# A selective-scan layer on one core: B and C loaded to 64 partitions and copied to the other 64 by ScalarE, u loaded in two halves

## The chip, the core and the metric

The kernel runs on one core of a Trainium2 chip. The metric is the device time of one execution in microseconds (us); lower is better. Engines are named as in the profile: PE is TensorE's matmul side and PEld its weight loads, DVE is VectorE, ACT is ScalarE, POOL is GpSimd, SP is SyncE, which only issues DMAs here.

## The reference, cut to what matters

The network has four layers on an input of 2 x 128 x 128 x 128 (images, channels, rows, columns): a Mamba layer (layer 0), a gate made from 8 x 8 windows (layer 1), a second Mamba layer of the same form (layer 2) and a residual block of two 3x3 convolutions (layer 3). The change is in the Mamba layers alone. After a 3x3 convolution, the 128 channels of every pixel are read as a sequence of 8 tokens with 16 features:

```python
seq = y.reshape(B * H * W, 8, 16)
xz = einsum('nld,ed->nle', seq, in_proj_w); xi, z = split(xz, 2)     # 32 inner channels each
xc = silu(causal_conv4(xi) + conv1d_b)
dt, Bm, Cm = split(einsum('nld,ed->nle', xc, x_proj_w), [1, 17])     # 1, 16 and 16 wide
dt = softplus(einsum('nlr,dr->nld', dt, dt_proj_w) + dt_proj_b)
dA, dBx = exp(dt[..., None] * A), dt[..., None] * Bm[:, :, None, :] * xc[..., None]
h = dA * h + dBx;  y_t = sum(h * C_t, over the 16 states)            # scan over the 8 tokens
out = einsum('nld,ed->nle', (y + D * xc) * silu(z), out_proj_w)
```

Each pixel has its own sequence, with a state h of 32 inner channels x 16 states. After the layer comes a group norm, SiLU and the residual.

## The kernel before, in words

One tile is 4 image rows, 512 pixels; `_mamba` handles 64 tiles for each of the two layers, numbered k. The state of a token is a tile of 128 partitions x 4 x 512: the 32 inner channels are split into 4 groups j (`NJ`, on the free axis) of 8 channels e (`DJ`), and the 128 partitions are the 8 channels e x 16 states n. Which partition holds which (e, n) is told by `_state` (L72), and the constant matrices `neg`, `red` and `alog` are laid out by it.

For every tile, PE and ACT make xc, z, dt, B and C, all with pixels on the free axis, through one PSUM buffer `one`: a matmul writes it, ACT copies it out, and the next matmul may start. POOL makes u = dt * xc (L374). As u, B and C are needed on other partitions than where they arise, `store` (L376) writes them to scratch in DRAM (`su` and `sb`, ten DMAs), and `load` (L429) reads them back for each of tokens 0 to 6, replicated over partitions: u to all 16 states n (`ur`, 128 x 4 x 512), and B and C to all 8 channels e (`bcr`, 128 x 2 x 512). Before the change a load is four DMAs on SP, in this order: u to partitions 0 to 111 (L435), u to 112 to 127 (L436), B and C to 0 to 111 (L439), B and C to 112 to 127 (L440). `ur` has 3 buffers, `bcr` 5.

Then, for each token t:

- `inject` (L442, POOL, instruction L445) makes h_t = ur * B, for t = 0 to 6, in one instruction of 128 x 2048. `h` has 4 buffers.
- `decay` (L447), for t = 1 to 7: eight matmul pieces (L454) spread dt over the partitions and scale it by A, into two PSUM tiles `set` of 128 x 1024; ACT takes exp of each (L463). There are three `set` buffers, so ACT can be at most one and a half tokens ahead of DVE.
- `token` (L465), twice per token, once for each half of the 2048 columns: DVE multiplies the set by the state before (L472), multiplies that by C into `r` (L473) and, but for the last token, adds the injected part (L477).
- `gather` (L485): PE sums `r` over the states into `ys` (L492).

`gate` (L501, DVE instruction L505), `out` (L507, with L512 and L520), `spread` (DVE, L523) and `keep` (SP, L527) finish a tile.

The order on every engine is written by hand: each step is put on a list with a due time in tokens, tile k adding 7k (`SPAN`); the list is sorted, and each engine runs its part of it in that order. In a due time t is the token. What matters here: `load` is due at t - 3.7, `inject` at t - 1.8, `decay` at t - 1.2, `token` at t - 1. Around the end of a tile's scan ACT therefore has, in this order and partly for the next tiles: exp of token 6 (both halves), the copy of z's second half (L354), a table load, SiLU of xc and of z (L357), the copy of B (L407), a table load, exp of token 7, a copy of dt (L365), the copy of C (L407), exp of the next tile's token 1, a second copy of dt (L365). On the next token's period follow copies of `t` (L421) and of `o` (L520), exp of token 2, a table load, softplus (L368), a table load and exp of token 3. PE's matmuls L400 (for B and C), L364 (for dt) and L454 stand between these, each waiting for ACT to clear `one`.

SP's DMAs signal on eight semaphores in turn, and an issue waits for the DMA eight before it to land; so at most eight DMAs, two loads, are under way.

Of the kernel before, what the change touches and what calls it, by code (L numbers as in the profile page):

```python
# [31 lines left out]
P = 128  # L32
NT, FT = 8, 16
DI, DS, DC = 32, 16, 4
NQ = 4
NJ = DI * DS // P
DJ = DI // NJ
NG = 4
CG = P // NG
WIN = 8  # L40
ROWS = 4
NS = ROWS * P
# [7 lines left out]
def _constants(H):  # L50

    parts = {}

    neg = np.zeros((NJ, NQ, DJ, NQ, P), np.float32)
    red = np.zeros((P, NQ, NQ, DJ), np.float32)
    gsum = np.zeros((2, NQ, DS, 2, NJ, NQ, DJ), np.float32)
    for q in range(NQ):
        for e in range(DJ):
            neg[:, q, e, q, _state(e)] = -1.0
            red[_state(e), q, q, e] = 1.0  # L60
        for g in range(2):
            gsum[g, q, :, g, :, q, :] = 1.0
    parts["neg"] = neg.reshape(P, -1)
    parts["red"] = red.reshape(P, -1)
    parts["gsum"] = gsum.reshape(P, -1)
    parts["group"] = np.kron(np.eye(NG), np.full((CG, CG), 1.0 / CG)).astype(np.float32)
    parts["ident"] = np.eye(P, dtype=np.float32)
    parts["neghalf"] = np.full((P, CG), -0.5, np.float32)
    return _packed(parts)


def _state(e):  # L72


    return np.arange(DS) + P - DS if e == DJ - 1 else np.arange(DS) * (DJ - 1) + e


def _bilinear(n):
# [38 lines left out]
def _mamba_layout(w):  # L117
# [5 lines left out]
    def half(a):  # L123

        a = a.reshape(*a.shape[:-2], 2, NQ, NJ, DJ)
        return np.ascontiguousarray(np.swapaxes(a, -3, -2)).reshape(*a.shape[:-4], 2 * P)
# [18 lines left out]
    for q in range(NQ):  # L145
        pdt1[:, q, :, :, q, :] = by_d[0][:, :, None, None]
        pdt2[:, q, :, :, q, :] = w["dt_proj_w"][:, 0].reshape(NJ, DJ)[None, None, :, :]
        pb[:, q, :, q, :] = by_d[1 : 1 + DS].transpose(1, 2, 0)
        pc[:, q, :, q, :] = by_d[1 + DS :].transpose(1, 2, 0)
        for e in range(DJ):  # L150
            alog[:, q, e, q, _state(e)] = w["A_log"].reshape(NJ, DJ, DS)[:, e, :]
# [126 lines left out]
OWN_AT = (-6.3, -5.8)  # L278
U_AT, OWN_U_AT = -5.0, -4.3
STORE_AT = -4.15  # L280
LOAD_AT, INJECT_AT = -3.7, -1.8
REP_AT = -1.2
SUM_AT = 0.35
D_AT = (1.25, 4.2)
# [4 lines left out]
def _mamba(tc, src, w, con, dst, scratch, stats, H):  # L289


    nc = tc.nc
# [11 lines left out]
    live = {}  # L304
# [124 lines left out]
    def load(k, t):  # L429

        s = live[k]
        n = P - DS
        ur = s["ur", t] = st.tile([P, NJ, NS], F32, tag="ur", name="ur", bufs=3)
        u = s["su"][t]
        nc.sync.dma_start(out=ur[:n], in_=u[: DJ - 1].unsqueeze(0).to_broadcast([DS, DJ - 1, NJ, NS]))  # L435
        nc.sync.dma_start(out=ur[n:], in_=u[DJ - 1].unsqueeze(0).to_broadcast([DS, NJ, NS]))  # L436
        m = s["bc", t] = st.tile([P, 2, NS], F32, tag="bcr", name="bcr", bufs=5)
        b = s["sb"][t]
        nc.sync.dma_start(out=m[:n], in_=b.unsqueeze(1).to_broadcast([DS, DJ - 1, 2, NS]))  # L439
        nc.sync.dma_start(out=m[n:], in_=b)  # L440

    def inject(k, t):  # L442
        s = live[k]
# [90 lines left out]
    def taps(k, a, b):  # L534
        return [(k, conv, tap) for tap in range(a, b)]
# [11 lines left out]
    x1, z1 = ahead(1)[0], behind(1)[0]  # L547
    order = [(0, band)] + taps(0, 0, 9) + [(0, turn)] + x0 + taps(1, 0, 3) + dt0 + taps(1, 3, 5) + bc0
    order += [(0, load, 0), (0, load, 1), (0, load, 2)]
    order += z0 + taps(1, 5, 9) + [(1, turn), (0, decay, 1), (0, inject, 0), (0, inject, 1)] + own0  # L550
    order += x1[:2] + z1[:2]
    early = {x: n - 100.0 for n, x in enumerate(order)}

    def put(k, at, f, *args):
        at = early.get((k, f, *args), k * SPAN + at)
        todo.append((at, len(todo), f, (k, *args)))


    for k in range(len(src) * ntile):
        if k * ROWS % BAND == 0:  # L560
            put(k, BAND_AT, band)
        for tap in range(9):
            put(k, CONV_AT[tap], conv, tap)
        put(k, TURN_AT, turn)
        for n in range(4):
            put(k, IN_AT[n], project, *divmod(n, 2))
        for name in ("xc", "zs"):
            put(k, SILU_AT, silu, name)
        for i in range(2):
            put(k, BC_AT[i], inout, i)  # L570
        for g in range(2):
            put(k, DT_AT[g], step, g)
        put(k, SOFTPLUS_AT, softplus)
        put(k, PROD_AT, product)
        put(k, U_AT, scaled)
        for g in range(2):
            put(k, OWN_AT[g], own, g)
        put(k, OWN_U_AT, own_u)
        put(k, STORE_AT, store)
        for t in range(NT - 1):  # L580
            put(k, LOAD_AT + t, load, t)
            put(k, INJECT_AT + t, inject, t)
        for t in range(1, NT):
            put(k, REP_AT + t, decay, t)
            for jp in range(2):
                put(k, t - 1 + jp / 2, token, t, jp)
            put(k, SUM_AT + t, gather, t)
        for g in range(2):
            put(k, D_AT[g], through, g)
            put(k, V_AT[g], gate, g)  # L590
        put(k, OUT_AT, out)
        put(k, STATS_AT, spread)
        put(k, KEEP_AT, keep)
# [26 lines left out]
def _gates(tc, src, w, con, y, stats, wm, b1, up, dst, H):  # L620
# [6 lines left out]
    with tc.tile_pool(name="dg", bufs=2) as dp, tc.tile_pool(name="dg1", bufs=1) as sp, tc.tile_pool(  # L627
# [58 lines left out]
        def gram(b, y0):  # L686
# [3 lines left out]
            pg = s["pg"] = psg.tile([P, 2, 512], F32, tag="pg", name="pg")  # L690
            tiles = [(a, a * P // 2, g * CG) for g in range(NG) for a in range(2)]
            for a, pa, c0 in tiles:
# [335 lines left out]
def _program(ctx, tc, d, cols, out):  # L1028
# [7 lines left out]
    with tc.tile_pool(name="const", bufs=1) as cp, tc.tile_pool(name="wts", bufs=1) as wp:  # L1036
        cc = cols["const"]
        ct = cp.tile([P, cc["neghalf"][1]], F32, tag="ct", name="ct")
        nc.sync.dma_start(out=ct, in_=d["const"])
        con = {k: ct[:, a:b] for k, (a, b) in cc.items()}  # L1040
        w1 = cp.tile([P, CG], F32, tag="w1", name="w1")
        nc.sync.dma_start(out=w1, in_=d["w1t"])
        w2 = cp.tile([CG, 2 * P + P // 2], F32, tag="w2", name="w2")
        nc.sync.dma_start(out=w2, in_=d["w2b"])
        b1 = cp.tile([CG, 1], F32, tag="b1", name="b1")
        nc.sync.dma_start(out=b1, in_=d["b1"])
        wm = {"w1": w1, "w2": w2[:, :P], "b2": w2[:, P : 2 * P], "one": w2[:, 2 * P :]}

        y = [dram.tile([P, H, P], F32, tag=f"y_{b}", name=f"y_{b}") for b in range(B)]

        def layer(src, n):
            w = _layer_weights(nc, wp, {k: d[f"L{n}_{k}"] for k in ("conv", "fold", "alog", "keep")}, cols[n], con)
            stats = wp.tile([P, B, H // ROWS, 6], F32, tag="stats", name="stats")
            _mamba(tc, src, w, con, y, scratch, stats, H)
            return w, stats

        x = [d["x"][b] for b in range(B)]
        w, stats = layer(x, 0)
        _gates(tc, x, w, con, y, stats, wm, b1, d["up"], x2, H)
        w, stats = layer(x2, 2)  # L1060
        with tc.tile_pool(name="ps_n", bufs=1, space=PSUM) as pp:
            norm = [_norm(nc, npool, pp, w, con, stats, b) for b in range(B)]
# [44 lines left out]
```

## Time and profile before

| what | value |
|---|---|
| time, median of 3 runs | 7559.09 us (7551.93 to 7567.43) |
| span of the profiled execution | 7571.5 us |
| DVE busy in the span | 7011.8 us (93%) |
| POOL, PE, ACT busy in the span | 73%, 83%, 57% |
| DMA | 1769.80 MB, mean 234 GB/s |
| layer 0's scan, first to last DVE token instruction | 57 to 3307 us |
| layer 2's scan | 3655 to 6899 us |

The profiled execution has no separate time of its own; its span is 12.4 us above the median of the three runs, so a profiled microsecond is taken as a run's microsecond, and differences are added to the median. The profile gives, for each engine, its busy time, the groups of instructions by source line with the idle time just before them and what ended it ("releaser"), a table of waits, a timeline of instructions, and tables of busy time by window with the granted TensorE clock and the share of time that the 16 DMA engines were busy. The scan stages of the two layers are 6493 us of the span and the rest is the gate layer, the residual block and the start.

### The profile page before, as it was taken

Reading aid. Unit: us, or ns where it says so; the run is one execution under the profiler, and the core shown is the slowest. Engines: PE = TensorE matmul, PEld = TensorE weight load, DVE = VectorE, ACT = ScalarE, POOL = GpSimd, SP = SyncE. Lnnn points to the kernel's source line nnn. Section 1 sums busy time; section 2 is a strip of 40 time slices with the busy share of each in tenths; the row PEclk is TensorE's granted clock in tenths of the full one; section 3 lists DMA queues with packets and bytes.
Section 4 is the critical chain, followed back from the end, with each engine's and each line's share of the span. In section 5 each row is a group of like instructions: output and inputs, shape, how many; then the busy total and the mean of one; then the engine's idle time right before and its main releaser. Section 6 shows DMA issues by size and latency. Waiting matters only on the chain.

```text
span 7571.5 us, 89536 instructions
## 1 busy us (share of the span) xinstructions
PE 6319.0 (83%) x30416; PEld 2335.1 (31%) x30416; DVE 7011.8 (93%) x7114; ACT 4282.3 (57%) x4877; POOL 5499.8 (73%) x1783
## 2 busy tenths in 40 slices
PE   7888888888888888867788888888888888887994
PEld 2222222222222222224222222222222222223873
DVE  5999999999999999978699999999999999999986
ACT  5666666666656656545556666666656655662222
POOL 5878777877787778754578777877787778775541
PEclk8999999999999999978899999999999999997997
DMA  8999999999999999954799999999999999996604
GB/s 204 252 251 252 251 250 246 256 251 253 246 248 254 250 243 249 245 194 173 193 249 247 250 250 249 250 256 246 249 252 252 251 245 253 249 253 199 207 7 172
DMA packets 573738, 1769.80 MB, mean 234 GB/s; under 512 B 85568, under 2 KB 239712, under 8 KB 458208
## 3 DMA queue, kind: packets, MB, share of 16 engines
q1 hardware_dynamic: 568672, 1747.28, 88.1%
q10 hardware_dynamic: 4608, 16.78, 0.6%
q8 instruction: 242, 3.96, 0.2%
q14 instruction: 216, 1.77, 0.1%
HBM read 1552.83 MB, written 210.89 MB: 233 GB/s over the span
## 4 chain that ended last, share of the span: by engine, by line
DVE 41%; DMA 25%; PE 19%; issue 7%; ACT 5%; POOL 2%; SPq 1%; POOLq 0%; DVEq 0%; ACTq 0%
DMA bcr<-sb 19%; DVE set L472 14%; DVE h L477 12%; DVE r L473 12%; PE m L911 6%; DMA ur<-su 3%; PE one L350 2%; PE set L454 2%; ACT set L463 2%; PE ys L492 2%; PE one L400 2%; POOL h L445 2%; DVE v L505 1%; PE ys L483 1%; ACT xc L357 1%
## 5 line engine op out<-in xcount | busy, mean ns | idle before, releaser
L445 POOL TENSOR_TENSOR h<-ur,bcr 128x2048 f32<-128x2048 f32 x896 | 4060.7, 4539 | 1257.0 <-DMA bcr<-sb 1096.1
L472 DVE TENSOR_TENSOR set<-set,h 128x1024 f32<-128x1024 f32 x1792 | 2193.5, 1224 | 267.6 <-ACT set L463 165.4
L473 DVE TENSOR_TENSOR r<-set,bcr 128x1024 f32<-128x1024 f32 x1792 | 2194.5, 1225 | 61.5
L463 ACT ACTIVATE set<-set 128x1024 f32<-128x1024 f32 x1792 | 1745.9, 1006 | 870.0 <-PE set L454 856.6
L477 DVE TENSOR_TENSOR h<-set,h 128x1024 f32<-128x1024 f32 x1536 | 1866.0, 1215 | 28.1 <-POOL h L445 27.8
L454 PE MATMUL set<-dt,rep 32*128 32x512 f32 x7168 | 1402.9, 675 | 104.9 <-DVE h L477 98.1
L492 PE MATMUL ys<-r,ct 128*32 128x512 f32 x7168 | 1172.5, 635 | 36.4 <-DVE r L473 36.1
L323 PE MATMUL one<-band,conv 128*128 128x512 f32 x2304 | 1081.3, 605 | 21.9 <-DMA band<-in_x_dram 12.6
L454 PEld LDWEIGHTS set<-dt,rep 32*128 32x128 f32 x7168 | 405.1, 193 | 1002.3 <-issue 468.1
L400 PE MATMUL one<-xc,keep 128*64 128x512 f32 x1008 | 322.4, 723 | 462.1 <-ACT xc L357 355.5
L323 PEld LDWEIGHTS one<-band,conv 128*128 128x128 f32 x2304 | 406.6, 189 | 668.0 <-issue 596.8
L911 PE MATMUL m<-comb,u 128*128 128x256 f32 x2304 | 507.8, 381 | 46.0 <-DVE comb L904 44.8
L483 PE MATMUL ys<-t,ct 128*128 128x512 f32 x512 | 322.6, 716 | 252.3 <-DVE v L505 250.7
L911 PEld LDWEIGHTS m<-comb,u 128*128 128x128 f32 x2304 | 436.2, 190 | 117.3 <-issue 54.5
L492 PEld LDWEIGHTS ys<-r,ct 128*32 128x32 f32 x7168 | 181.2, 112 | 929.2 <-issue 759.6
L352 ACT ACTIVATE xc<-one,keep 128x512 f32<-128x512 f32 x252 | 173.4, 688 | 509.2 <-PE one L350 504.2
L374 POOL TENSOR_TENSOR u<-dt,xc 128x1024 f32<-128x1024 f32 x128 | 302.8, 2365 | 98.0 <-ACT dt L368 98.0
L420 PE MATMUL one<-prod,ct 128*128 128x512 f32 x504 | 280.8, 640 | 109.1 <-POOL prod L412 78.8
L350 PE MATMUL one<-y,w_in 128*128 128x512 f32 x504 | 341.1, 765 | 1.6 <-ACT xc L352 1.6
L463 ACT ACT_TABLE_LOAD x254 | 325.9, 1283 | 4.5
L427 POOL TENSOR_TENSOR t<-t,xc 128x1024 f32<-128x1024 f32 x128 | 302.4, 2363 | 10.0
L364 PE MATMUL one<-xc,w_dt 128*128 128x512 f32 x504 | 306.4, 692 | 2.7 <-ACT bc L407 2.7
(167 smaller groups left out, 5901.7 us busy)
## 6 DMA issues: line engine op xcount, KB each, us to landing
ur<-su SPq DMA_DIRECT2D x896, 896.0 KB, 11.5
bcr<-sb SPq DMA_DIRECT2D x896, 448.0 KB, 11.7
ur<-su SPq DMA_DIRECT2D x896, 128.0 KB, 11.1
su<-u SPq DMA_DIRECT2D x1024, 64.0 KB, 3.4
sb<-bc SPq DMA_DIRECT2D x256, 224.0 KB, 2.7
bcr<-sb SPq DMA_DIRECT2D x896, 64.0 KB, 11.0
y<-o SPq DMA_DIRECT2D x128, 256.0 KB, 9.3
band<-in_x_dram SPq DMA_DIRECT2D x28, 640.0 KB, 10.9
```

Of the source, the lines that this page charges most:

```text
L323: nc.tensor.matmul(py.rearrange("p (r w) -> p r w", r=ROWS), lhsT=w["conv"][:, tap, :], rhs=xb[:, r + kh : r + kh + ROWS, kw : kw + P], st ...
L350: nc.tensor.matmul(p, lhsT=w[("in", "z")[i]][:, g, :], rhs=s["y"], start=True, stop=True)
L400: nc.tensor.matmul(p[g * NQ * DS : (g + 1) * NQ * DS, :], lhsT=w[("xb", "xcm")[i]], rhs=s["xc"][:, g, :], start=True, stop=True,)
L445: nc.gpsimd.tensor_tensor(b, s["ur", t], s["bc", t][:, 0].unsqueeze(1).to_broadcast([P, NJ, NS]), ALU.mult)
L454: nc.tensor.matmul(a[j // 2][:, j % 2, :], lhsT=w["rep"][r, q, :], rhs=s["dt"][r, g, :], start=True, stop=True, tile_position=(r.start, 0),)
L463: nc.scalar.activation(x, x, AF.Exp)
L472: nc.vector.tensor_tensor(pt, pt, s["h", t - 1][:, js, :], ALU.mult)
L473: nc.vector.tensor_tensor(s["r", t][:, js, :], pt, s["bc", t - 1][:, 1].unsqueeze(1).to_broadcast([P, 2, NS]), ALU.mult)
L477: nc.vector.tensor_tensor(s["h", t][:, js, :], pt, s["h", t][:, js, :], ALU.add)
L483: nc.tensor.matmul(s["ys", g], lhsT=con["ident"], rhs=s["t1"][:, g, :], start=True, stop=False)
L492: nc.tensor.matmul(s["ys", g][a : a + NQ * DJ, :], lhsT=red[:, q, :], rhs=r[:, j, :], start=False, stop=(q == NQ - 1), tile_position=(0, a),)
L911: nc.tensor.matmul(m[:, n // 2, n % 2], lhsT=u[:, i, kw, :], rhs=v[:, i, :, kw : kw + P], start=(kw == 0), stop=(kw == 2),)
```

## The change

`_state` gets a new order of partitions: channel e and state n sit on partition 64 * (e // 4) + 4 * n + e % 4, so that the lower 64 partitions hold channels 0 to 3 and the upper 64 hold channels 4 to 7. As B and C do not depend on the channel, the two halves of `bcr` are then equal. `load` reads B and C for partitions 0 to 63 only, by two DMAs of 32 partitions whose source has 8 states as its leading dimension, and a new step `double` copies them to partitions 64 to 127 with one ACT instruction of 64 x 1024. u is loaded by two DMAs of 64 partitions, the upper half first; its bytes stay the same. A load still has four DMAs, but B and C now come before u. `double` is due at t - 2.19, just behind the exp of the token before (due at t - 2.2) and ahead of `inject` (t - 1.8), which reads its result, as `token` does.

```diff
+NE = DJ // 2
 def _state(e):
-    return np.arange(DS) + P - DS if e == DJ - 1 else np.arange(DS) * (DJ - 1) + e
+    return P // 2 * (e // NE) + NE * np.arange(DS) + e % NE
...
-LOAD_AT, INJECT_AT = -3.7, -1.8
+LOAD_AT, DOUBLE_AT, INJECT_AT = -3.7, -2.19, -1.8
...
     def load(k, t):
         s = live[k]
-        n = P - DS
+        half, part = P // 2, P // 4
         ur = s["ur", t] = st.tile([P, NJ, NS], F32, tag="ur", name="ur", bufs=3)
-        u = s["su"][t]
-        nc.sync.dma_start(out=ur[:n], in_=u[: DJ - 1].unsqueeze(0).to_broadcast([DS, DJ - 1, NJ, NS]))
-        nc.sync.dma_start(out=ur[n:], in_=u[DJ - 1].unsqueeze(0).to_broadcast([DS, NJ, NS]))
         m = s["bc", t] = st.tile([P, 2, NS], F32, tag="bcr", name="bcr", bufs=5)
-        b = s["sb"][t]
-        nc.sync.dma_start(out=m[:n], in_=b.unsqueeze(1).to_broadcast([DS, DJ - 1, 2, NS]))
-        nc.sync.dma_start(out=m[n:], in_=b)
+        u, b = s["su"][t], s["sb"][t]
+        for at in (0, part):
+            rows = b[at // NE : (at + part) // NE]
+            nc.sync.dma_start(
+                out=m[at : at + part], in_=rows.unsqueeze(1).to_broadcast([part // NE, NE, 2, NS])
+            )
+        for at, e in ((half, NE), (0, 0)):
+            nc.sync.dma_start(
+                out=ur[at : at + half], in_=u[e : e + NE].unsqueeze(0).to_broadcast([DS, NE, NJ, NS])
+            )
+
+    def double(k, t):
+        m = live[k]["bc", t]
+        nc.scalar.copy(m[P // 2 :], m[: P // 2])
...
+            put(k, DOUBLE_AT + t, double, t)
             put(k, INJECT_AT + t, inject, t)
```

In the first tile's hand-made order, `double` of tokens 0 and 1 is put just before the steps that need it.

More of the change, by code (lines that the diff above doesn't have):

```diff
@@ L549, in _mamba @@
     order += [(0, load, 0), (0, load, 1), (0, load, 2)]
-    order += z0 + taps(1, 5, 9) + [(1, turn), (0, decay, 1), (0, inject, 0), (0, inject, 1)] + own0
+    order += z0 + taps(1, 5, 9) + [(1, turn), (0, double, 0), (0, decay, 1), (0, inject, 0), (0, double, 1), (0, inject, 1)] + own0
     order += x1[:2] + z1[:2]
```

## Prediction

> **What bounds the kernel now.** First the table of busy time by window, for a stretch inside layer 2's scan. Columns: window, length, busy us of PE, PEld, DVE, ACT and POOL, granted clock, DMA share, GB/s.
>
> ```profile
> 5000.00:6400.00 1400.00, 1194.37 (x4950) 377.26 (x4942) 1353.10 (x1197) 856.08 (x974) 1109.30 (x322) 0.96 0.98 250
> ```
>
> Two things are nearly full: DVE, 1353 of 1400 us, and the DMA engines, 0.98 of the time at 250 GB/s. A tile takes (3307 - 57) / 64 = 50.8 us, so DVE's 46.9 idle us over 27.6 tiles are 1.7 us per tile: the most that could ever be won is 1.7 x 128 = 218 us, 2.9%. The DMA engines work 0.98 x 50.8 = 49.8 us per tile. Then the waits (engine and line, released by: us in total, times, longest):
>
> ```profile
> POOL h L445 <- DMA bcr<-sb: 1096.1, 406, 14.4
> ...
> DVE set L472 <- ACT set L463: 165.4, 185, 9.3
> ...
> DVE set L472 <- POOL h L445: 97.2, 2, 51.8
> ...
> DVE h L477 <- POOL h L445: 27.8, 24, 3.6
> ```
>
> POOL waits for loads often, but that reaches DVE (last line) in 27.8 us only; the 97.2 us are the two layers' starts. What holds DVE up is exp (L463). Where, the ACT timeline tells, at the end of tile 38's scan (start, us, operation, [idle before]):
>
> ```profile
> 2020.36 1.93 ACT L463 ACTIVATE set<-set 128x1024 f32<-128x1024 f32 x2 [0.48 <-PE set L454]
> 2022.19 0.60 ACT L354 COPY zs<-one 128x512 f32<-128x512 f32 x1
> 2022.81 1.28 ACT L357 ACT_TABLE_LOAD   x1
> 2024.11 1.06 ACT L357 ACTIVATE xc<-xc 128x1024 f32<-128x1024 f32 x1
> 2025.07 1.04 ACT L357 ACTIVATE zs<-zs 128x1024 f32<-128x1024 f32 x1
> 2026.34 0.59 ACT L407 COPY bc<-one 128x512 f32<-128x512 f32 x1 [0.23 <-PE one L400]
> 2026.95 1.28 ACT L463 ACT_TABLE_LOAD   x1
> 2028.24 1.93 ACT L463 ACTIVATE set<-set 128x1024 f32<-128x1024 f32 x2
> 2030.07 0.69 ACT L365 ACTIVATE dt<-one,keep 128x512 f32<-128x512 f32 x1
> 2031.93 0.59 ACT L407 COPY bc<-one 128x512 f32<-128x512 f32 x1 [1.18 <-PE one L400]
> 2032.99 1.92 ACT L463 ACTIVATE set<-set 128x1024 f32<-128x1024 f32 x2 [0.47 <-PE set L454]
> ```
>
> The pairs are exp of token 6, of token 7 and of the next tile's token 1. DVE's first use of each, on its own timeline:
>
> ```profile
> 2022.14 1.22 DVE L472 TENSOR_TENSOR set<-set,h 128x1024 f32<-128x1024 f32 x1
> ...
> 2029.80 1.22 DVE L472 TENSOR_TENSOR set<-set,h 128x1024 f32<-128x1024 f32 x1
> ...
> 2034.59 1.22 DVE L472 TENSOR_TENSOR set<-set,h 128x1024 f32<-128x1024 f32 x1
> ```
>
> The first exp of a pair takes 1.01 us, so the leads (exp done before DVE needs it) are 0.77, 0.55 and 0.59 us. This is one of the best tiles. Laying both timelines side by side over all tiles, the median lead is 0.03 us at tokens 6 and 7 and 0.10 at token 1, against 2.9, 1.2, 1.2 and 3.4 at tokens 2 to 5. ACT is 39% idle on average and still just in time at three places of the tile.
>
> **The copies on ACT.** 7 per tile, 896 in all, each 64 x 1024 from SBUF to SBUF. Not in this trace; rows around it: COPY of 128x512 0.59 us (L354), ACTIVATE of 128x1024 1.04 to 1.15 us (L357, L426). 512 more columns cost 1.04 - 0.60 = 0.44 with SiLU, so I take 0.59 + 0.43 = 1.02 us, ends 0.59 and 1.15. Neighbours overlap by 0.09 us (the exp pair: 1.93 for 2 x 1.01), so a copy shifts what is behind it by s = 0.93 (ends 0.50 and 1.06). Below nothing is excluded: it takes no work off ACT. By the order of instructions each copy stands just behind an exp pair, of tokens 6, 7 (of the tile before) and 1 to 5. What is behind each:
>
> - Behind token 6's pair: z's copy, table load, SiLU, B's copy, table load, exp 7, with no idle but 0.23 us. From the start of exp 6 to the end of the first exp 7 are 8.89 us, while DVE needs 7.66 us from token 6 to token 7. Every us goes through: 0.93 in tiles without lead, 0.93 - 0.55 = 0.38 in the quarter of tiles with one. Mean 0.75 x 0.93 + 0.25 x 0.38 = 0.79 us.
> - Behind token 7's pair: dt's copy, which PE's second L400 waits for, then C's copy, decay 1, exp 1. From exp 7 to exp 1 are 4.75 us, DVE needs 4.79. So 0.93 - 0.04 = 0.89 us more, in all tiles, on top.
> - Behind token 1's: lead 2.9 us, covered. Behind 2, 3, 4: the next ACT instruction waits 0.97 (o, for PE), 0.91 (xc, for POOL's u) and 0.98 us (yc, for PE), covered within 0.02. Behind 5: xc's copy, whose matmul successor waits 1.95 us for DVE's gate, covered. If these covers went, each would cost up to 0.93 x 126 = 117 us.
>
> Sum: 1.68 us per tile, over the 126 tiles that follow another: **+212 us** (ends 105 and 245).
>
> **PE's clock.** While ACT does SiLU, PE stands still for 2.83 us (L400 waits for xc). In some tiles the granted clock is then half:
>
> ```profile
> 2119.07:2125.90 6.83, 4.00 (x22) 0.83 (x22) 6.03 (x6) 5.47 (x7) 1.37 (x1) 1.00 1.01 253
> 2125.90:2129.31 3.41, 3.41 (x12) 0.73 (x12) 3.38 (x4) 2.29 (x3) 3.23 (x2) 0.50 1.02 259
> ```
>
> In this tile (40) B's copy waits 1.10 instead of 0.23 us for L400 and DVE waits 1.00 us at token 7: about 0.85 us more. 51 of 128 tiles have it. The copy ahead of SiLU makes PE's pause 3.8 us. If all tiles got it, 77 x 0.85 = +65; if none, -43. I take 32 more tiles, **+27 us**.
>
> **The loads.** u keeps its 1024 KB per load; B and C go from 512 to 256 KB. DMA traffic falls by 896 x 256 KiB = 235 MB, 1.84 MB of a tile's 12.7. On the busiest engines it may not fall at all: if both B-C transfers run on the same eight of 16, these carry 1024/16 + 256/8 = 96 KB per load, as now (1536/16). So a tile needs between 49.8 us x 10.9/12.7 = 42.7 and 49.8 us of DMA time, under a tile of 52.5 us: loads stop being late. Today DVE's idle outside tokens 6 and 7 and the two first tiles, mostly a late inject of token 1 and what it delays, is some 60 us in both layers; the first tiles lose another 25. Ends 0 and -85; I take **-50 us**, as a tile of 52.5 us needs these loads later anyway.
>
> The Trainium skill speaks against the halves: "SBUF — State Buffer", section "Door 1: The DMA port swizzle", says that 64 partitions reach 8 of 16 ports, and measured 196 GB/s against 328 for 128. By that, u would take 5.3 us of a load instead of 3.2; no row here shows a load of 64 partitions.
>
> B and C now come first on SP. Their issue waits for DVE's L473 of four tokens ago (a wait that is there today: 222.9 us in total), and u is behind it; for token 0 it waits for sb's DMAs, so that u is issued 3.7 us later (B and C go out at 2013.4 and 2014.0 today, so u at 2014.5 instead of 2010.8). Inject 0 ends 7 us (median) before DVE needs it: covered. The new wait is ACT's, for B and C to land. Today bcr lands, by token, between 1.6 us before and 1.3 us after the end of the exp pair that the copy follows (medians), with u ahead of it; without 1024 KB ahead, at 250 GB/s, it lands some 4 us earlier, so the copy rarely waits. POOL's inject now waits for the copy: inject 1 starts 1.0 us behind exp 7's pair, ends 5.6 behind it, and DVE's L477 comes 7.4 behind it with the delays above. The order of states changes only constants: nothing.
>
> **Sum.** 212 + 27 - 50 = +189 us, added to the median: 7559 + 189 = **7748 us**.
>
> **Rivals.**
> - *Copies wait for B and C* (the loads not relieved, or as late as now). The positive part of the landings is about 1.1 us at token 0's copy and 0.3 at token 1's, the two exposed places: 1.4 x 126 = 176, and no relief: 7748 + 176 + 50 = 7974. For it: POOL's 406 waits. Against it: the new order on SP.
> - *The new pattern is slower on the DMA engines.* From below 10.9 MB / 52.3 us = 208 GB/s loads set the tile. At 193 GB/s, the lowest of the short windows that I asked for (2112 to 2115.6, DMA share 0.66, so partly idle), a tile is 56.5 us: 5.7 x 126 = +718, 8277. Against it: 253 to 293 GB/s in the windows behind it.
> - *Faster*: the copies fall wholly into ACT's idle 39% and the relief stays: -60, 7500. It decides if the two exposed places lose under 0.2 us each, which needs the chain from exp 6 to exp 7 to be set by PE rather than by ACT's own instructions. The list above, with 0.23 us idle in 8.89, says no.
> - *The change does nothing*: copies hidden, DMA's busiest engines as before: 7559.
>
> **Chances.** Forecast 0.70 (7640 to 7870 by the copy's ends and the clock's), copies waiting 0.10, slow pattern 0.08, faster 0.10, nothing 0.02. The range 7640 to 7950 leaves out the slow pattern, the faster case and half of the waiting one. A measurement of this kernel can tell about 0.2% from no change. Faster by more 0.10; within 0.03 (the last case and the forecast's lowest edge); slower 0.87.
>
> **What would show it.** L472's wait for L463 rises from 165 to about 380 us, at tokens 7 and 1; a group of 896 ACT copies of about 1.0 us, with little idle before them; POOL's L445 waits for ACT instead of bcr; DVE busy stays at 7012; 1535 MB of DMA at some 200 GB/s; a tile of about 52.3 us. Wrong if the copies' group shows idle released by bcr, if the DMA share stays at 0.98 with longer tiles, or if the leads at tokens 7 and 1 do not shrink.

## The result, and the profile after

The changed kernel takes 7819.3 us (median of 4 runs, 7818.45 to 7822.24), the kernel before on the same chip 7563.26 (4 runs): a ratio of 1.0335, 95% interval 1.032 to 1.0349. The forecast was 7748, in 7640 to 7950. The profiled executions have spans of 7571.5 and 7816.7 us, so the working below accounts for +245.2 us. The medians of the runs differ by 256.0 us; most of the rest is that the profiled execution of the kernel before was itself some 10 us longer than its median.

Line numbers have moved: exp is L473 (was L463), DVE's three instructions are L482, L483, L487 (L472, L473, L477), inject is L455 (L445), B's and C's copy L408 (L407), the matmuls ahead of it L401 (L400), the new copy L450. First the same window as before, same columns:

```profile
5000.00:6400.00 1400.00, 1133.06 (x4771) 365.91 (x4770) 1306.92 (x1155) 1024.84 (x1126) 1073.12 (x312) 0.93 0.73 206
```

The DMA engines went from 0.98 to 0.73 of the time; DVE lost 46 us of its work in this window, about 3.3%. A tile now takes 52.35 us instead of 50.6. Three of the costliest groups (busy us, mean ns of one, idle time before them and its main releaser):

```profile
L482 DVE TENSOR_TENSOR set<-set,h 128x1024 f32<-128x1024 f32 x1792 | 2193.7, 1224 | 535.7 <-ACT set L473 435.5
...
L455 POOL TENSOR_TENSOR h<-ur,bcr 128x2048 f32<-128x2048 f32 x896 | 4058.6, 4536 | 1610.4 <-ACT bcr L450 960.1
...
L450 ACT COPY bcr<-bcr 64x1024 f32<-64x1024 f32 x896 | 934.6, 1043 | 38.0 <-DMA bcr<-sb 16.5
```

The copies take 1.04 us and hardly ever wait. The waits table:

```profile
POOL h L455 <- ACT bcr L450: 960.1, 265, 5.5
...
DVE set L482 <- ACT set L473: 435.5, 348, 20.8
...
POOL h L455 <- DMA bcr<-sb: 126.6, 42, 5.5
...
DVE set L482 <- POOL h L455: 100.2, 2, 53.1
...
DVE h L487 <- POOL h L455: 6.1, 2, 4.1
```

POOL's wait for B and C fell from 1096 to 127 us, and a wait for ACT stands in its place. DVE's L487 waits for POOL for 6.1 us, where it was 27.8. DVE's wait for exp grew from 165.4 to 435.5. ACT's timeline at the end of a tile (start, us, operation, [idle before]), with the copies in it:

```profile
5087.20 1.93 ACT L473 ACTIVATE set<-set 128x1024 f32<-128x1024 f32 x2 [0.48 <-PE set L464]
5089.15 1.04 ACT L450 COPY bcr<-bcr 64x1024 f32<-64x1024 f32 x1
5090.22 0.58 ACT L355 COPY zs<-one 128x512 f32<-128x512 f32 x1
5090.82 1.28 ACT L358 ACT_TABLE_LOAD   x1
5092.12 1.06 ACT L358 ACTIVATE xc<-xc 128x1024 f32<-128x1024 f32 x1
5093.08 1.04 ACT L358 ACTIVATE zs<-zs 128x1024 f32<-128x1024 f32 x1
5094.73 0.58 ACT L408 COPY bc<-one 128x512 f32<-128x512 f32 x1 [0.61 <-PE one L401]
5095.33 1.28 ACT L473 ACT_TABLE_LOAD   x1
5096.74 1.93 ACT L473 ACTIVATE set<-set 128x1024 f32<-128x1024 f32 x2
5098.69 1.04 ACT L450 COPY bcr<-bcr 64x1024 f32<-64x1024 f32 x1
5099.76 0.69 ACT L366 ACTIVATE dt<-one,keep 128x512 f32<-128x512 f32 x1
5101.62 0.58 ACT L408 COPY bc<-one 128x512 f32<-128x512 f32 x1 [1.18 <-PE one L401]
5102.68 1.93 ACT L473 ACTIVATE set<-set 128x1024 f32<-128x1024 f32 x2 [0.47 <-DVE r L483]
```

and DVE's first use of the three exp pairs:

```profile
5093.11 1.22 DVE L482 TENSOR_TENSOR set<-set,h 128x1024 f32<-128x1024 f32 x1
...
5097.78 1.23 DVE L482 TENSOR_TENSOR set<-set,h 128x1024 f32<-128x1024 f32 x1 [1.06 <-ACT set L473]
...
5103.79 1.23 DVE L482 TENSOR_TENSOR set<-set,h 128x1024 f32<-128x1024 f32 x1 [1.12 <-ACT set L473]
```

DVE waits at tokens 7 and 1, as the prediction said. One thing differs from its working: the copy starts 0.02 us after its neighbour's end and its successor 0.03 us after its own. Before, z's copy began 1.83 us after the start of its exp pair (2022.19 - 2020.36); now it begins 3.02 us after (5090.22 - 5087.20). The copy shifts what is behind it by 1.19 us, not by 0.93.

To see all tiles, I took the intervals between the starts of DVE's 1792 instructions of L482, less the undisturbed interval of that place in a tile (3.53 us; 4.13 where one more short instruction stands between; 2.41 behind a half of token 7, which has no add). What is left is DVE's waiting, by the place where it shows: the sum over tiles 1 to 63 of both layers, in us of the profiled execution (the first tiles have a column of their own).

| kernel | span | two first tiles | token 7 | token 1 | token 6 | token 3 | late injects (second half of tokens 1 and 5, token 2) |
|---|---|---|---|---|---|---|---|
| before | 7571.5 | 25.4 | 63.4 | 10.4 | 72.8 | 15.7 | 36.4 |
| after | 7816.7 | 50.4 | 207.2 | 145.9 | 37.4 | 25.8 | 1.9 |
| difference | +245.2 | +25.0 | +143.8 | +135.5 | -35.4 | +10.1 | -34.5 |

The differences sum to 244.5. These columns serve for the experiments too.

### The profile page after: what moved, and what is told of

It reads as the page before. It is cut to its first block, busy times and chain, and to the rows that moved or that the text cites. A ratio compares the mean times of both kernels' runs of the same rounds, so it can differ in the third digit from the quotient of the medians.

```text
span 7816.7 us, 91356 instructions
## 1 busy us (share of the span) xinstructions
PE 6219.2 (80%) x30416; PEld 2339.7 (30%) x30416; DVE 7013.5 (90%) x7114; ACT 5235.2 (67%) x5773; POOL 5500.8 (70%) x1783
## 2 busy tenths in 40 slices
DMA packets 502072, 1534.97 MB, mean 196 GB/s; under 512 B 71232, under 2 KB 225376, under 8 KB 386528
## 4 chain that ended last, share of the span: by engine, by line
DVE 38%; PE 27%; ACT 13%; DMA 11%; issue 6%; SPq 3%; POOL 2%; ACTq 0%; DVEq 0%; POOLq 0%
DVE set L482 13%; DVE r L483 11%; DVE h L487 10%; PE m L922 6%; DMA ur<-su 6%; PE set L464 5%; ACT set L473 5%; PE one L351 3%; ACT bcr L450 3%; PE one L401 2%; PE ys L502 2%; PE ys L493 2%; DMA y<-o 2%; ACT L358 2%; SPq L439 2%
## 5 line engine op out<-in xcount | busy, mean ns | idle before, releaser
L455 POOL TENSOR_TENSOR h<-ur,bcr 128x2048 f32<-128x2048 f32 x896 | 4058.6, 4536 | 1610.4 <-ACT bcr L450 960.1
L482 DVE TENSOR_TENSOR set<-set,h 128x1024 f32<-128x1024 f32 x1792 | 2193.7, 1224 | 535.7 <-ACT set L473 435.5
L483 DVE TENSOR_TENSOR r<-set,bcr 128x1024 f32<-128x1024 f32 x1792 | 2194.3, 1225 | 61.4
L473 ACT ACTIVATE set<-set 128x1024 f32<-128x1024 f32 x1792 | 1737.6, 1007 | 736.4 <-PE set L464 657.6
L487 DVE TENSOR_TENSOR h<-set,h 128x1024 f32<-128x1024 f32 x1536 | 1864.6, 1214 | 6.1 <-POOL h L455 6.1
L464 PE MATMUL set<-dt,rep 32*128 32x512 f32 x7168 | 1367.8, 731 | 84.1 <-DVE h L487 81.4
L502 PE MATMUL ys<-r,ct 128*32 128x512 f32 x7168 | 1039.7, 631 | 8.1 <-DVE r L483 8.1
L450 ACT COPY bcr<-bcr 64x1024 f32<-64x1024 f32 x896 | 934.6, 1043 | 38.0 <-DMA bcr<-sb 16.5
L401 PE MATMUL one<-xc,keep 128*64 128x512 f32 x1008 | 360.3, 800 | 652.6 <-ACT xc L358 502.8
L464 PEld LDWEIGHTS set<-dt,rep 32*128 32x128 f32 x7168 | 375.0, 202 | 922.8 <-issue 549.6
L493 PE MATMUL ys<-t,ct 128*128 128x512 f32 x512 | 293.4, 655 | 312.7 <-DVE v L515 250.0
L922 PEld LDWEIGHTS m<-comb,u 128*128 128x128 f32 x2304 | 436.9, 191 | 117.9 <-issue 54.5
L502 PEld LDWEIGHTS ys<-r,ct 128*32 128x32 f32 x7168 | 155.6, 110 | 789.9 <-issue 751.5
L365 PE MATMUL one<-xc,w_dt 128*128 128x512 f32 x504 | 355.0, 793 | 2.7 <-ACT bc L408 2.7
L522 PEld LDWEIGHTS po<-keep,v 128*128 128x128 f32 x2048 | 295.4, 230 | 129.2 <-DVE v L515 57.9
## 6 DMA issues: line engine op xcount, KB each, us to landing
y<-o SPq DMA_DIRECT2D x128, 256.0 KB
```

What stands on the lines that cost most here:

```text
L401: nc.tensor.matmul(p[g * NQ * DS : (g + 1) * NQ * DS, :], lhsT=w[("xb", "xcm")[i]], rhs=s["xc"][:, g, :], start=True, stop=True,)
L450: nc.scalar.copy(m[P // 2 :], m[: P // 2])
L455: nc.gpsimd.tensor_tensor(b, s["ur", t], s["bc", t][:, 0].unsqueeze(1).to_broadcast([P, NJ, NS]), ALU.mult)
L464: nc.tensor.matmul(a[j // 2][:, j % 2, :], lhsT=w["rep"][r, q, :], rhs=s["dt"][r, g, :], start=True, stop=True, tile_position=(r.start, 0),)
L473: nc.scalar.activation(x, x, AF.Exp)
L482: nc.vector.tensor_tensor(pt, pt, s["h", t - 1][:, js, :], ALU.mult)
```

## The experiments

**My theory**: the whole loss is that of copies standing on ACT between exp pairs that DVE awaits; the lighter loads bring little, as a longer tile hides them anyway. **Rivals**: the loads by halves are slower (slow pattern), or POOL's wait for the copy delays injects.

### 1. The loads alone, without copies

The changed kernel with u by halves and the new order of states, but B and C loaded to all 128 partitions by two transfers of 64, and no copies.

```diff
-        for at in (0, part):
-            rows = b[at // NE : (at + part) // NE]
-            nc.sync.dma_start(
-                out=m[at : at + part], in_=rows.unsqueeze(1).to_broadcast([part // NE, NE, 2, NS])
-            )
+        for at in (0, half):
+            nc.sync.dma_start(out=m[at : at + half], in_=b.unsqueeze(1).to_broadcast([DS, NE, 2, NS]))
...
-            put(k, DOUBLE_AT + t, double, t)
```

> New order of states and u by halves, but B and C are loaded for all 128 partitions by two DMAs of 64, and there is no copy on ACT. If the loss comes from ACT's copies: no slower than the kernel before, 7500 to 7570 us, with the irregular waits of DVE (36 us in the profile of before) partly gone. If the halves themselves are slower on the DMA engines, as the rival of the slow pattern says: over 7650 us and a DMA share of 0.98. The granted share tells whether halves carry a byte faster or slower: before it was 0.98 at 250 GB/s.

Measured: 8467.9 us, 1.1187 (1.1169 to 1.1205). My expectation was wrong by a long way. The window, and the group of inject:

```profile
5000.00:6400.00 1400.00, 1095.22 (x4344) 352.77 (x4343) 1192.83 (x1048) 749.51 (x852) 971.84 (x283) 0.88 0.95 219
```

```profile
L447 POOL TENSOR_TENSOR h<-ur,bcr 128x2048 f32<-128x2048 f32 x896 | 4056.0, 4532 | 2307.2 <-DMA ur<-su 1827.4
```

The engines are as good as full (0.95) and move 219 GB/s, where the kernel before moved 250 at 0.98, with the same 1769.80 MB. Loads by halves are slower, so the slow pattern of the prediction exists; in the changed kernel, with fewer bytes, it does not set the tile. This run also has the change's order of the four DMAs, B and C first; a run of halves in the old order was not made, so how much of the loss is the order's stays open. The Trainium skill's rule that spoke against the halves ("SBUF — State Buffer", section "Door 1: The DMA port swizzle", 196 GB/s against 328) points the right way; its size, 40% less, was not met here, where two loads are under way and 219 of 250 GB/s are left.

### 2. The copies alone

The kernel before with seven copies per tile at the places of the change's copies. They read a constant and write a buffer that nobody reads, 64 x 1024 from partitions 0 to 63 to 64 to 127.

```diff
+    def double(k, t):
+        m = st.tile([P, 2, NS], F32, tag="spare", name="spare", bufs=1)
+        c = w["conv"].rearrange("p a b -> p (a b)")[:, : 2 * NS].rearrange("p (a b) -> p a b", a=2)
+        nc.scalar.copy(m[P // 2 :], c[: P // 2])
...
+            put(k, DOUBLE_AT + t, double, t)
```

> The kernel before with its old loads, and seven ACT copies of 64 x 1024 per tile added at the due times of the change, from a weight tile to a spare tile that nobody reads, so that they wait for no load and nobody waits for them. If the place of the copies in ACT's order is the cause: as slow as the changed kernel or slower, 7790 to 7870 us, with waits for exp at tokens 7 and 1 as there. If the loss came from waiting for B and C or from POOL waiting for the copy: under 7650 us.

Measured: 7794.62 us, 1.0295 (1.0279 to 1.031). The two groups:

```profile
L478 DVE TENSOR_TENSOR set<-set,h 128x1024 f32<-128x1024 f32 x1792 | 2194.0, 1224 | 511.1 <-ACT set L469 412.4
...
L446 ACT COPY spare<-conv 64x1024 f32<-64x1024 f32 x896 | 934.7, 1043 | 21.5
```

By place: token 7 205.9, token 1 150.0, token 6 35.2, token 3 26.0, late injects 2.1, first tiles 31.9. That is the changed kernel's table but for the first tiles. So the copies alone make the loss but for some 20 us, with the old loads and no wait of POOL for a copy. And the late injects vanish here as well, at 1769.85 MB and a DMA share of 0.92: the longer tile relieves the loads, and the 235 MB that the change saves add nothing to that.

### 3. The same copies without crossing partitions

```diff
-        nc.scalar.copy(m[P // 2 :], c[: P // 2])
+        nc.scalar.copy(m[: P // 2], c[: P // 2])
```

> As the run of copies only, but from partitions 0 to 63 to the same partitions 0 to 63. In the changed kernel a copy of 1.04 us shifts what is behind it by 1.19 us, since it overlaps neither neighbour (others overlap by 0.09 us). If that comes from reading and writing different partitions: the overlap returns, and this run is some 2 x 0.2 x 126 = 50 us faster than the run of copies only. If it comes from any copy from SBUF to SBUF at this place: the same time.

Measured: 7658.15 us, 1.0113 (1.0096 to 1.013): 136.5 us less than with the copies that cross, where I had expected some 50. The copy itself is as long as the crossing one; its neighbours are not where they were. The group, and the timeline around token 7's pair:

```profile
L446 ACT COPY spare<-conv 64x1024 f32<-64x1024 f32 x896 | 927.9, 1036 | 0.0
```

```profile
5087.56 1.93 ACT L469 ACTIVATE set<-set 128x1024 f32<-128x1024 f32 x2
5089.39 1.04 ACT L446 COPY spare<-conv 64x1024 f32<-64x1024 f32 x1
5090.32 0.69 ACT L365 ACTIVATE dt<-one,keep 128x512 f32<-128x512 f32 x1
```

From the pair's start to dt's copy are 2.76 us; in experiment 2 they are 3.02 (5088.38 to 5091.40), before 1.83. In place, the copy shifts by 0.93 us, exactly the prediction's number; crossing, by 1.19. By place: token 7 126.5, token 1 117.9, token 6 27.1, token 3 1.9, late injects 6.9. Against experiment 2 that is 79 us less at token 7, 32 at token 1 and 24 at token 3.

Part of token 7's difference is PE's clock. While ACT does SiLU, PE pauses, and in the tiles where its clock is granted at half behind the pause (0.50 in the last microsecond before B's copy, as in the prediction's tile 40), B's copy (L407) waits about 1.13 us for PE instead of 0.23. Of 126 tiles, over 0.9 us are waited in 55 before (the prediction had counted 51), 79 after, 80 in experiment 2 and only 51 here. Another 45 tiles after and 42 in experiment 2 wait between, as the 0.61 us of the timeline above; before and here none does. The mean wait is 0.62, 0.92, 0.92 and 0.61 us, so of the 79 us at token 7 some 0.31 x 126 = 39 are the clock's. PE's pause is 2.83 us before, 4.01 in the changed kernel and in experiment 2, and 3.74 here: the copy in place lengthens it and brings no tile more, the crossing copy brings 24 or 25. But the length of the pause alone does not set their number: experiments 4 and 5 have the pause of before, 2.83 us, and 4 and 33 such tiles. What else sets it, and why a copy to other partitions does not overlap its neighbours, the runs do not tell.

### 4. One copy moved

In the changed kernel, only token 0's copy (behind exp of token 6) goes to an earlier place, ahead of z's first copy.

```diff
-            put(k, DOUBLE_AT + t, double, t)
+            put(k, -2.7 if t == 0 else DOUBLE_AT + t, double, t)
```

> The changed kernel with token 0's copy alone moved, from behind exp of token 6 to the idle time between the second copy of xc and the first of z. If each exposed copy has its own price: DVE's waits at token 7 fall from 207 us to the 63 us of before or below, those at token 1 stay near 146 us, and the time is some 144 us under the changed kernel, 7660 to 7700 us. If the two places share one cause, the wait moves on to token 1: over 7780 us.

Measured: 7674.55 us, 1.0129 (1.0104 to 1.0154). Token 7's wait falls from 207.2 to 25.4, token 1's stays (144.2), token 3's falls from 25.8 to 1.5, and token 6's rises from 37.4 to 102.9, where the copy is now ahead of exp 6. Each copy's price sits where its place is, and part of it moves with it. The long waits of B's copy fall to 4 of 126 tiles.

### 5. Two copies moved

```diff
+DOUBLE_AT = (-2.7, -0.7) + tuple(t - 2.19 for t in range(2, SPAN))
...
-            put(k, INJECT_AT + t, inject, t)
+            put(k, -0.65 if t == 1 else INJECT_AT + t, inject, t)
```

> The changed kernel with two of seven copies moved on ACT: token 0's from behind exp of token 6 to the idle time between the second copy of xc and the first of z (1.36 us), token 1's from behind exp of token 7 to the idle time between the copy of dt and the copy of C (1.18 us), with inject 1 right behind it. If these two places are the cause: the 279 us at tokens 7 and 1 go, 7530 to 7600 us. If ACT's total work, POOL's waits or the loads are the cause: over 7750 us.

Measured: 7675.5 us, 1.0136 (1.0121 to 1.0151), no better than moving one; the expected time was missed. Tokens 7 and 1 are down to 27.1 and 10.5, but token 2 has 60.3 and token 3 124.5 instead. As the trace of one tile reads, the new wait comes through POOL: token 1's copy now stands behind dt's, inject 1 waits for it, and `prod`, which follows inject 1 on POOL, is late with it. Token 1's copy on ACT, then POOL's inject 1, `prod` and inject 2:

```profile
5098.45 1.04 ACT L451 COPY bcr<-bcr 64x1024 f32<-64x1024 f32 x1
```

```profile
5099.57 4.54 POOL L456 TENSOR_TENSOR h<-ur,bcr 128x2048 f32<-128x2048 f32 x1 [7.10 <-DMA bcr<-sb]
5104.06 1.28 POOL L414 TENSOR_TENSOR prod<-bc 128x512 f32<-128x512 f32 x1
5105.29 4.53 POOL L456 TENSOR_TENSOR h<-ur,bcr 128x2048 f32<-128x2048 f32 x1
```

```profile
PEld one L422 <- POOL prod L414: 403.2, 124, 3.5
...
PE one L422 <- POOL prod L414: 290.6, 124, 2.6
```

Inject 1 starts at 5099.57, 0.08 us after the copy ends at 5099.49, although the profile puts its wait down to a DMA. `prod` runs behind it, and PE's L422 waits for `prod` in 124 tiles (before: PEld 138.2 us in 60, PE 78.8 in 42). In the same tile ACT's copy of `t` then waits 3.14 us for L422, and exp 2 stands behind it. Over the whole run that copy waits 338.0 us for PE, where the changed kernel has 175.0. So this is a new wait in the place of two that were removed; no run moves inject 1 or `prod` alone, so the chain is read from the trace and not tested.

### 6. All copies in ACT's idle times, loads split

Copies at seven chosen places; B and C of token 1 loaded ahead of u of token 0; and in each layer's first tile the copies behind the work for D and the next tile.

```diff
+DOUBLE_AT = (-2.9, -2.7, -0.7, 0.5, 1.81, 2.81, 3.81)
...
+            put(k, LOAD_AT + t - (t == 1) * 0.999, load, t)
+            put(k, LOAD_AT + t + 0.002, load_u, t)
+            put(k, DOUBLE_AT[t], double, t)
```

> The changed kernel with its copies in idle times of ACT: token 0's between the two copies of xc, token 1's between xc and z, token 2's between the copies of dt and C, token 3's behind the second copy of dt; 4 to 6 as they are. So that token 1's has landed, B and C of token 1 are loaded ahead of u of token 0. In the first tile the copies stand behind what they held up. If the place in ACT's order is the whole price, the waits at tokens 7, 1, 2 and 3 are those of before or less and the relief of the loads (36 us) and more is left: 7480 to 7560 us, faster than both kernels. If ACT's total work or the loss of overlap at a copy matters by itself: over 7600 us.

Measured: 7556.45 us (12 runs) against 7572.85 of the kernel before on the same chip (17 runs): 0.9972 (0.9959 to 0.9985), faster than both kernels, than the one before by about 0.3%. Its window and its wait for exp:

```profile
5000.00:6400.00 1400.00, 1206.62 (x4956) 379.29 (x4956) 1355.30 (x1201) 1062.19 (x1170) 1115.62 (x324) 0.96 0.78 214
```

```profile
DVE set L488 <- ACT set L479: 155.2, 163, 11.5
```

ACT does the same 896 copies, and DVE's wait for exp is back below that of before (165.4). By place: token 7 61.6, token 1 7.1, token 6 83.4, token 3 1.5, late injects 4.6, first tiles 26.3. Against before the late injects and token 3 have lost 46 us of waits, of which token 6 takes 11 back and the later starts of the two scans 10 (62.0 instead of 57.4 us from the start to the first L488, 354.8 instead of 349.4 between the layers). That is some 30 us in this profile, taken from the shortest of the 12 runs; the medians differ by 16 us (11 to 31 by the interval). So with the copies out of the way, the lighter loads and the orders chosen with them bring that much together; a version with these copies and the old loads was not run, so what each of them brings stays open.

### 7. B and C in one transfer of 64 partitions

```diff
-        for at in (0, part):
-            rows = b[at // NE : (at + part) // NE]
-            nc.sync.dma_start(
-                out=m[at : at + part], in_=rows.unsqueeze(1).to_broadcast([part // NE, NE, 2, NS])
-            )
+        nc.sync.dma_start(out=m[:half], in_=b.unsqueeze(1).to_broadcast([DS, NE, 2, NS]))
```

> The changed kernel with B and C for the lower 64 partitions in one DMA of 64 partitions whose leading dimension is 16, instead of two DMAs of 32 partitions with 8; copies and u as in the changed kernel, the same bytes. If the shape of these two DMAs keeps the halves of u from hindering each other: the DMA share rises from 0.73 to over 0.9 at about 206 GB/s, as in the run of halves without copies (0.95 at 219 GB/s), and the time is a little longer, 7820 to 7950 us. If the smaller bytes alone brought the DMA share down: 0.73 again and 7819 us.

Measured: 7820.62 us, 1.0317 (1.0294 to 1.034), the changed kernel's time within the intervals.

```profile
5000.00:6400.00 1400.00, 1132.12 (x4790) 364.85 (x4786) 1309.58 (x1158) 1029.01 (x1129) 1072.57 (x311) 0.93 0.87 207
```

With the same bytes in the same time the DMA engines are busy 0.87 instead of 0.73 of it, between the two values expected. So the form with 8 states leading does take a sixth off the DMA engines' time, and none of it shows in the kernel's time, since no load is awaited where the copies set the pace.

### 8. Four transfers of 32 partitions, no copies

```diff
-        for at in (0, part):
-            rows = b[at // NE : (at + part) // NE]
+        for at in (0, part, half, half + part):
+            rows = b[at % half // NE : (at % half + part) // NE]
...
-            put(k, DOUBLE_AT + t, double, t)
```

> New order of states, u by halves, B and C for all 128 partitions by four DMAs of 32 partitions whose leading dimension is 8; no copies; 512 KB of B and C again. If such a DMA always runs on the same eight engines, these carry 1024/16 + 512/8 = 128 KB per load where the other eight carry 64, so the mean DMA share stays at or under about 0.75 while POOL waits for loads; over 7700 us. If the DMAs spread over all engines, 96 KB each: share over 0.9, as in the run of halves.

Measured in one run: 7952.85 us. POOL waits for u for 1174.4 and for B and C for 260.6 us.

```profile
5000.00:6400.00 1400.00, 1156.46 (x4662) 366.15 (x4660) 1278.60 (x1127) 804.59 (x915) 1046.52 (x304) 0.91 0.77 236
```

Loads are late here and still the mean busy share is only 0.77. That fits transfers which all run on the same half of the engines, so that these are full while the others idle: u gives each of 16 engines 1024 / 16 = 64 KB per load, B and C give each of eight 512 / 8 = 64 KB more, so the mean would be (1 + 0.5) / 2 = 0.75. The profile does not give the engines one by one, so this is an inference from the share. The trace's records of landings fit it: each transfer of 32 partitions has 9 of them, here and in the changed kernel, every other DMA of SP 16. The Trainium skill says the same in "DMA: Bandwidth & Descriptors", section "Why a DMA increments its semaphore by 16 and not by 1": a transfer is spread over the largest number up to 16 that divides both slowest dimensions, from the lowest-numbered engine on. The share here agrees with it. Yet at 236 GB/s it is quicker than experiment 1 at 219.

### 9. The first tile's order alone

```diff
-    order += z0 + taps(1, 5, 9) + [(1, turn), (0, double, 0), (0, decay, 1), (0, inject, 0), (0, double, 1), (0, inject, 1)] + own0
-    order += x1[:2] + z1[:2]
+    order += z0 + taps(1, 5, 9) + [(1, turn), (0, decay, 1)] + own0[:2] + [(0, double, 0), (0, inject, 0)]
+    order += x1[:2] + [(0, double, 1), (0, inject, 1)] + own0[2:] + z1[:2]
```

> The changed kernel with one edit: in each layer's first tile, the copies of tokens 0 and 1 stand behind the work for D and the next tile that they hold up there, instead of ahead of it. Theory (about 25 us of the loss come from ACT, which stands still for those two loads with other work queued behind it): the waits of the two first tiles fall from 50 to some 27 us and the time from 7819 to about 7797; all other waits stay. Rival (the loads land later in the first tiles by their new order on SP): the waits stay near 50 us and the time near 7819.

Measured: 7807.71 us, 1.0287 (1.0271 to 1.0303; before 7584.48 on that chip). The first tiles' waits fall from 50.4 to 35.9, all other places stay within 2.5 us. What was removed can be read in the changed kernel's ACT timeline of the first tile:

```profile
48.71 1.04 ACT L450 COPY bcr<-bcr 64x1024 f32<-64x1024 f32 x1 [5.37 <-DMA bcr<-sb]
49.77 1.28 ACT L473 ACT_TABLE_LOAD   x1
51.07 1.93 ACT L473 ACTIVATE set<-set 128x1024 f32<-128x1024 f32 x2
55.38 1.04 ACT L450 COPY bcr<-bcr 64x1024 f32<-64x1024 f32 x1 [2.39 <-DMA bcr<-sb]
56.45 0.58 ACT L422 COPY t<-set 128x512 f32<-128x512 f32 x1
```

ACT stands 5.37 and 2.39 us for the first loads to land, with the rest of its first tile queued behind the copies; DVE pays at token 2: in that tile it waits 20.75 us there, where it waited 9.28 before. So 14.5 of the 25.0 us are the place of these two copies. Of the other 10.5 I cannot say more than that experiment 6, which also loads in another order, does not have them.

## Why the prediction was right, point by point

The direction, the mechanism and the two places were right. The sum was 189 us and the profile has 245.2; by its terms:

| term | forecast | measured |
|---|---|---|
| copies at tokens 7 and 1, with PE's clock | +212 + 27 = +239 | +143.8 + 135.5 = +279.3 |
| loads and first tiles | -50 | -34.5 + 25.0 = -9.5 |
| tokens 6 and 3 | none | -35.4 + 10.1 = -25.3 |

- **Length and shift of a copy.** The length was right (1.02 forecast, 1.04 measured), the shift was the term that was mis-sized. "Neighbours overlap by 0.09" was read from instructions that stay on their partitions; the copy that crosses them overlaps with neither neighbour, 1.19 us instead of 0.93 and above the upper end of 1.06. With 1.19 the prediction's own formulas give (0.75 x 1.19 + 0.25 x 0.64) x 126 = 133 at token 7 and 1.15 x 126 = 145 at token 1, 278 in all. The in-place copies of experiment 3, with 0.93, added 63.1 + 107.5 = 171, where the same formulas give 212. So they price a copy somewhat too high, and that 278 meets the 279.3 measured is partly luck.
- **PE's clock.** Forecast 32 more tiles and 27 us; measured 24 more and, by the mean wait of B's copy, 0.30 x 126 = 38 us. It is part of token 7's number. That it came near is luck: the prediction reasoned from a pause of 3.8 us, and experiment 3, with 3.74, has 51 such tiles, fewer than before. The 278 above and these 38 would be 316, more than the 279.3 seen, so the leads have grown somewhat: token 6's waits fall as the tile waits elsewhere.
- **Token 6, -35.4.** Not foreseen. Experiment 2 shows the same (35.2 us left), so it belongs to the copies and not to the loads. The median lead of exp at token 6 grew from 0.03 to 0.77 us; that ACT catches up while DVE waits at tokens 7 and 1 is my reading of it, and no run isolates it.
- **The five covered copies.** Right by the waits: tokens 4 and 5 have none, and token 3's 10.1 us are all that shows. But the cover at token 3 was nearly used up: its median lead fell from 1.22 to 0.18 us. What lies behind a lost cover, experiment 5 shows: a wait of 124.5 us at token 3.
- **Loads.** The DMA share fell below the bound that I gave: 0.73 x 52.35 = 38.2 us per tile, where I had 42.7 to 49.8. The late injects did vanish (-34.5), though experiment 2 shows that they would have without lighter loads. What failed is the first tiles: expected within the -50, measured +25.0. Experiment 9 traces 14.5 of them to the place of two copies. I had weighed token 0's new order on SP and not that a copy which waits for a landing holds up ACT's whole queue.
- **The sum and the range.** Copies and clock were put 40 us too low and the loads' gain 40 us too high; the 25 us that tokens 6 and 3 gave back were in no term and made up for part of it, which is luck. The range's edges do not follow from the ends that are named: 7640 is 7559 + 105 + 27 - 50, with the clock's term in its middle (with its low end it would be 7571), and 7870 is 7559 + 245 + 65 with no relief by the loads.
- **The rivals.** The copies wait for B and C 16.5 us in all: in the trace, bcr lands, by token, 6.5 to 12.6 us (medians) before its copy starts, so that rival fell. The slow pattern is real (experiment 1) but not this kernel's bound, as its share of 0.73 shows. "Faster" needed places that lose under 0.2 us; experiment 6 has them, with copies elsewhere, and is 16 us faster than the kernel before where 60 were forecast.
- **What would show it.** L482's wait for exp 435.5 us (forecast 380), copies of 1.04 us, 1534.97 MB at 206 GB/s in the scan, a tile of 52.35 us (forecast 52.3): as said.

## What to carry to other kernels

An engine that is idle 40% of the time may have no free place just where a step is put: lay its instructions beside those of the engine that sets the pace, and put the price of a new instruction on the leads at that place. Relief of a resource that is nearly full is worth only the waits that reach the pacing engine, here about 35 us for a DMA share that fell by a quarter, and a tile that other work makes slower brings the same relief without the change. A new step that waits for a load belongs behind all work of its queue that does not need that load, in the first tile as well.

## What the runs showed of the hardware that was not expected

- A copy of 64 x 1024 on ACT from partitions 0 to 63 to 64 to 127 takes as long as one in place (1043 and 1036 ns), but starts 0.02 us after its predecessor's end, and its successor 0.03 us after its own; in place, both overlap by 0.1 us. Over 896 copies that made 136.5 us.
- Loads into halves of 64 partitions ran at 219 GB/s with the DMA engines 0.95 busy, against 250 GB/s at 0.98 for 112 and 16 partitions (in another order on SP); transfers of 32 partitions for B and C, with u still by halves, at 236 GB/s and a share of 0.77.
- Tiles in which PE comes out of the SiLU pause at half its clock did not grow in number with a copy that puts SiLU off by 0.93 us (51 of 126, before 55) and did with one that puts it off by 1.19 us (80). With the pause of before, 2.83 us, but other places of the copies they were 4 and 33 (experiments 4 and 5), so the pause alone does not set their number.
